# Role adapters on one core: every transfer of the phases on SyncE's queue, h as an image in DRAM, weight sums' transfers spread, tables loaded by place

## The chip, the cores and the metric

The kernel runs on one core of one Trainium2 chip. The metric is the device time of one execution in microseconds (us); the figure for the kernel before is the median of three executions.

## The reference

Two layers, each an adapter with a residual and a layer norm, whose weights are chosen per sample by a role (three roles; the drawn roles are 1 or 2). All data are float32; x has 128 samples of 128 x 1024.

```python
# one layer; role has one entry per sample, H = 1024, K = 512, R = 3
h = jnp.einsum('bsh,bhk->bsk', hidden_states, W_down[role]) + b_down[role][:, None, :]
h = jax.nn.gelu(h, approximate=False)
u = jnp.einsum('bsk,bkh->bsh', h, W_up[role]) + b_up[role][:, None, :]
y = hidden_states + u
mean = jnp.mean(y, axis=-1, keepdims=True)
var = jnp.mean(jnp.square(y - mean), axis=-1, keepdims=True)
yn = (y - mean) * jax.lax.rsqrt(var + LN_EPS)
return yn * gamma[role][:, None, :] + beta[role][:, None, :]
```

The second layer takes the first one's result and the same roles.

## The kernel before

**Sorting.** The kernel first counts the roles on the chip and orders the samples so that two of the same role stand side by side. An item is such a pair; 63 items are pairs, and item 63 holds the two samples left over. "Place" is the rank of a role: place 0 is the most frequent role, and weights and tables are stored by place.

**Phases and items.** The work is four phases: Down and Up of layer 0, then Down and Up of layer 1. In each, 64 items pass. Down makes h = gelu(x W_down + b) and stores h in DRAM (tensor hd); Up loads h and x, makes the product with W_up, adds x, normalises and stores to mid (layer 0) or to the result (layer 1).

**Seven products.** A pair is multiplied by Winograd's scheme: seven half-sized products instead of eight. It needs sums of quarters of the data (`winograd_sums`, mostly on GpSimd, POOL in the profile) and of the weights (T1 to T4). The products s1 to s7 of an item (`item_products`) accumulate into banks b, a and e. Bank b is used by s1, s3, s5 and s7 one after the other, and between them ScalarE (ACT) or VectorE (DVE) reads it: s7 may not start before DVE has read what s5 left (`end`, line 550). The sums of weights of the three later phases are made during the first phase by nine jobs (`Sums`, one for each phase and place): four transfers of 512 KB in, four subtractions on DVE (line 209), seven transfers of 512 KB out to DRAM (tensors B and T). They use the memory of tables 0 and 1.

**Layout of x and h.** [...] x is loaded by `quartered` in four pieces of 128 KB for a sample (line 384), into buffers with tag q, and DVE transposes it in blocks of 32 x 32 (line 522). h is stored row by row (line 558), loaded with `quartered` in four pieces of 64 KB for a sample, and transposed in Up (line 589).

**The order.** Every step has a time in a plan (`at`), in units; items start 7 units apart, so two of them overlap. The steps are written in the order of these times, and each engine keeps to that order. The times only set the order: an engine runs as early as the waits allow. In the plan of Down, the two halves of h are stored 10.7 and 12.5 units after the item's start; x is loaded 19 units ahead of an item in the first phase (fewer for the first four items) and 11.9 ahead in the third, and transposed 8.8 ahead.

**Queues.** A transfer is issued by SyncE (SP) or by ScalarE (ACT), each in its own order. Before, ACT issues the stores of h and the tables (bias, gamma, beta, three places in one go); SP issues the rest. Each transfer of either queue is given one of eight completion semaphores in turn (DMAHW0 to DMAHW7 in the listing of the order), and is issued only when the transfer before it on that semaphore has landed. So at most eight are under way, those of ACT among them.

**The end.** The last item's result is stored by `finish_last` in four pieces, three by SP (line 650) and one by ACT (line 656). Since the row of the result is known only at run time, each store into it waits for the one before.

Of the kernel before, what the change touches and what calls it, by code (L numbers as in the profile page):

```python
# [10 lines left out]
F32 = mybir.dt.float32  # L11
# [15 lines left out]
def kernel(  # L27
# [24 lines left out]


    nc = tc.nc
    B, S, H = x.shape
# [56 lines left out]
    def table(v, which):  # L112
        n = v.shape[1]
        t = tables[:, which].rearrange("p (r n) -> p r n", r=R)[:, :, 0:n]

        def load(places=range(R)):
            for k in places:
                r = reg(role_of, k, [ENG.Activation], R - 1)
                nc.scalar.dma_start(t[:, k], v[ds(r, 1), :].to_broadcast((P, n)))

        return t, load
# [53 lines left out]
    class Sums:  # L175
# [21 lines left out]

        def load(self):
            role = reg(role_of, self.k, [ENG.SP], R - 1)
            rows = self.w.shape[1] // NQ  # L200
            for q in range(NQ):
                src = self.w[ds(role, 1), ds(q * rows, rows), :]
                nc.sync.dma_start(
                    self.whole[ts(q, SQ)], src.rearrange("o (m i) c -> i (o m) c", i=SQ)
                )

# [7 lines left out]
    class Phase:  # L214
        def __init__(self, layer, up):
            self.layer, self.up, self.weights = layer, up, {}
            self.vectors = layers[layer][3:] if up else layers[layer][1:2]

        def load_bias(self, which):
            self.next_bias, load, self.subtract = bias_table(self.vectors[0], which)  # L220
            load()

        def set_bias(self):
            self.subtract()
            self.bias = self.next_bias

        def load_gamma(self):
            self.gamma, load = table(self.vectors[1], 1)
            load()

        def load_beta(self):
            self.beta, load = table(self.vectors[2], 2)
            load()

# [193 lines left out]
    def item_products(item, cols):  # L428
# [9 lines left out]
        if n < NPAIR:  # L438
# [61 lines left out]
    class Down:  # L500
# [18 lines left out]
        def prepare(self):  # L519
            self.a = flat("t", 3, "xT" + self.tag).rearrange("p (s j c) -> p s j c", s=2, c=P)  # L520
            for s in range(2):
                nc.vector.transpose(  # L522
                    self.a[:, s].rearrange("p j (a t) -> p j a t", t=SQ),
                    self.xq[s].rearrange("p a (j i) -> p j a i", i=SQ),
                )
                if s == 0 and self.early:
                    first_sum("T1", 0)
# [28 lines left out]
        def finish(self):  # L556
            return [
                (t, lambda s=s: nc.scalar.dma_start(hd[self.n][s], self.h[s]))
                for s, t in enumerate((10.7, 12.5))
            ]  # L560

    class Up:
# [63 lines left out]
        def finish_last(self):  # L626
# [3 lines left out]
            o = [flat("q", 4, f"o{self.tag}_{s}", H) for s in range(2)]  # L630
            out_row = lambda s: out[ds(self.out_at[s], 1)].rearrange("o s h -> (o s) h")
            row = lambda t, s, cols: t[:, ds(self.places[s], 1), cols].rearrange("p o n -> p (o n)")
# [14 lines left out]
            def stored(s, cols, queue):  # L647
                y, v = o[s][:, cols], mv[s][:, 2:3]
                nc.vector.scalar_tensor_tensor(y, y, v, row(self.ph.beta, s, cols), ALU.mult, ALU.add)  # L649
                queue.dma_start(out_row(s)[:, cols], y)  # L650

            def stored_beside():
                y, v = o[0][:, left], mv[0][:, 2:3]
                nc.scalar.mul(y, y, v)
                nc.gpsimd.tensor_tensor(y, y, row(self.ph.beta, 0, left), ALU.add)
                nc.scalar.dma_start(out_row(0)[:, left], y)

# [11 lines left out]
        def finish(self):  # L669
# [3 lines left out]
            for s in range(2):  # L673
# [22 lines left out]
                def stored(s=s, box=box, row=row):  # L696
# [6 lines left out]
                    if self.layer == 0:  # L703
                        dst = mid[self.n][s]
                    else:
                        i = reg(perm, 2 * self.n + s, [ENG.SP], B - 1)
                        dst = out[ds(i, 1)].rearrange("o s h -> (o s) h")
                    nc.sync.dma_start(dst, o)

# [17 lines left out]
    for k, ph in enumerate(phases):  # L727
# [36 lines left out]
        if k + 1 < len(phases):  # L764

            nxt = phases[k + 1]
            if nxt.up:
                at(base - 2 * SLOTS, lambda nxt=nxt: nxt.load_bias(0))
                at(base - 2 * SLOTS + 3, nxt.set_bias)
                at(base - 2 * SLOTS, nxt.load_gamma)  # L770
                at(base + 2 * SLOTS - 1, nxt.load_beta)
            else:


                at(base + 1.6, lambda nxt=nxt: nxt.load_bias(0))
                at(base + 4.2, nxt.set_bias)
                at(base + SLOTS * NI // 2, lambda nxt=nxt: nxt.load_bias(2))
                at(base + SLOTS * NI // 2 + 3, nxt.set_bias)

# [28 lines left out]
    at(-29, lambda: load_bias([0]))  # L808
    at(-29, lambda: load_rows(0, 0, nc.scalar, ENG.Activation, (0, 1)))
# [56 lines left out]
```

## Time and profile before

| what | value |
|---|---|
| median of three executions (range) | 3200.29 us (3198.03 to 3203.08) |
| the profiled execution, its own time | 3195.31 us |
| its span, first to last instruction | 3193.5 us |
| granted TensorE clock, mean | 0.994 |
| busy: PE / DVE / ACT / POOL | 3123.4 / 1762.3 / 1199.2 / 1767.4 us |
| DMA busy share, about: Down of layer 0 / Up of layer 0 / Down of layer 1 / Up of layer 1 | 0.76 / 0.71 / 0.47 / 0.67 |

PE is the matmul side of TensorE. A line of the view of waits reads: engine and line that waited, what it waited for, us in total, how often, the longest. A line of the timeline reads: start in us, length in us, engine, line, operation, output from input, how many in a row, and in brackets how long the engine had been idle and what ended that. SPq and ACTq are the two engines' instructions that issue transfers. A wait for a tensor named hd by SP is a wait for a store of h to land.

### The profile page before, as it was taken

The numbers are of one execution on the slowest core, as the hardware profiler recorded it, in microseconds if no ns is written. First come the engines' busy times: TensorE is split into PE (matmuls) and PEld (weight loads), VectorE is DVE, ScalarE is ACT, GpSimd is POOL, SyncE is SP. The second block draws the span as 40 slices with busy tenths as digits, with TensorE's granted clock in tenths as the row PEclk, the third lists the DMA queues.
The fourth block names the chain that finished last, engine by engine and source line by source line (L and its number), as shares of the span: only waits on it lengthen the run. The fifth ranks groups of instructions, "written<-read, shape, count | busy, mean of one in ns | idle before, by whom it ended". The sixth has DMA issues, their size and how long they took to land. (4 is left out here: it accounts for less than half of the span.)

```text
span 3193.5 us, 43475 instructions
## 1 busy us (share of the span) xinstructions
PE 3123.4 (98%) x10806; PEld 2054.9 (64%) x10806; DVE 1762.3 (55%) x2792; ACT 1199.2 (38%) x2814; POOL 1767.4 (55%) x1396
## 2 busy tenths in 40 slices
PE   8999999999999999999989999999999999999997
PEld 6888888888544444444478888888884444444443
DVE  4433333333577777777752332323226777787777
ACT  1222222222344545454432222222224545455453
POOL 3444434443467676777664433344435777677775
PEclk9999999999999999999999999999999999999999
DMA  6877777778887767677796444544468766666664
GB/s 154 204 215 212 202 206 203 207 203 230 273 252 214 220 211 218 210 223 213 224 258 172 133 129 132 142 130 135 128 182 290 242 211 223 219 211 227 211 220 165
DMA packets 447840, 642.87 MB, mean 201 GB/s; under 512 B 48497, under 2 KB 318322, under 8 KB 447602
## 3 DMA queue, kind: packets, MB, share of 16 engines
q1 hardware_dynamic: 406130, 559.85, 60.1%
q10 hardware_dynamic: 41472, 80.23, 7.2%
q8 instruction: 102, 1.67, 0.2%
q14 instruction: 136, 1.11, 0.1%
HBM read 405.54 MB, written 234.36 MB: 200 GB/s over the span
## 5 line engine op out<-in xcount | busy, mean ns | idle before, releaser
L407 PE MATMUL bu<-wall,hTu 128*128 (+1 forms) x2048 | 926.4, 594 | 17.3 <-DVE xu L611 12.2
L407 PEld LDWEIGHTS bu<-wall,hTu 128*128 128x128 f32 x2048 | 387.4, 190 | 513.9 <-issue 427.5
L398 POOL TENSOR_TENSOR Sd<-xTd 128x512 f32<-128x512 f32 x125 | 167.0, 1336 | 848.1 <-DVE xTd L522 776.1
L689 POOL TENSOR_TENSOR varu<-varu,mhalf 128x1 f32<-128x1 f32 x254 | 333.7, 1314 | 395.9 <-ACT varu L688 373.9
L522 DVE STREAM_TRANSPOSE xTd<-xqd 128x1024 f32<-128x1024 f32 x256 | 307.5, 1229 | 399.2 <-PE bd L407 259.9
L407 PE MATMUL bd<-wall,xTd 128*128 (+1 forms) x2080 | 493.1, 380 | 13.6 <-DVE hd L550 11.0
L692 DVE SCALAR_TENSOR_TENSOR ou<-xu,meanu,tables 128x1024 f32<-128x1024 f32 x254 | 326.2, 1284 | 317.6 <-ACT ou L687 317.6
L407 PE MATMUL eu<-wall,hTu 128*128 (+1 forms) x1040 | 488.4, 592 | 2.6 <-DMA wall<-T 1.5
L407 PE MATMUL bd<-wall,Sd 128*128 (+1 forms) x2016 | 477.9, 380 | 4.9 <-ACT hd L546 4.9
L407 PEld LDWEIGHTS bd<-wall,xTd 128*128 128x128 f32 x2080 | 395.3, 190 | 72.7 <-DVE hd L550 14.4
L407 PEld LDWEIGHTS bd<-wall,Sd 128*128 128x128 f32 x2016 | 384.0, 191 | 59.2 <-issue 7.0
L551 ACT ACTIVATE hd<-hd 128x256 f32<-128x256 f32 x382 | 157.5, 416 | 593.7 <-DVE hd L550 593.7
L407 PEld LDWEIGHTS eu<-wall,hTu 128*128 128x128 f32 x1040 | 197.3, 190 | 251.3 <-issue 239.6
L683 ACT ACTIVATE partu<-statu 128x2 f32<-128x2 f32 x254 | 51.7, 203 | 740.6 <-DVE xu L620 740.6
L700 POOL TENSOR_TENSOR ou<-ou,tables 128x1024 f32<-128x1024 f32 x127 | 298.9, 2354 | 0.0
L687 ACT ACTIVATE ou<-xu,meanu 128x1024 f32<-128x1024 f32 x254 | 291.7, 1148 | 13.7 <-DMA mid<-ou 5.2
L407 PE MATMUL ed<-wall,xTd 128*128 (+1 forms) x1072 | 254.0, 380 | 0.0
L398 POOL TENSOR_TENSOR hTu<-hTu 128x256 f32<-128x256 f32 x126 | 203.7, 1616 | 82.6 <-DVE hTu L589 63.1
L407 PE MATMUL ad<-wall,xTd 128*128 (+1 forms) x1008 | 240.0, 381 | 4.9 <-DMA wall<-in_L_cond_W_down_dram 4.9
L407 PE MATMUL ed<-wall,Sd 128*128 (+1 forms) x1008 | 238.1, 379 | 0.0
L407 PE MATMUL au<-wall,hTu 128*128 (+1 forms) x504 | 236.8, 592 | 0.0
L407 PEld LDWEIGHTS ed<-wall,xTd 128*128 128x128 f32 x1072 | 204.7, 191 | 28.7 <-ACT ou L687 0.2
(110 smaller groups left out, 3312.3 us busy)
## 6 DMA issues: line engine op xcount, KB each, us to landing
xqd<-in_x_dram SPq DMA_DIRECT2D x512, 128.0 KB, 3.2
hd<-hd ACTq DMA_DIRECT2D x256, 256.0 KB, 2.6
hqu<-hd SPq DMA_DIRECT2D x1024, 64.0 KB, 4.0
xu<-in_x_dram SPq DMA_DIRECT2D x128, 512.0 KB, 5.3
mid<-ou SPq DMA_DIRECT2D x128, 512.0 KB, 4.3
xqd<-mid SPq DMA_DIRECT2D x512, 128.0 KB, 3.4
xu<-mid SPq DMA_DIRECT2D x128, 512.0 KB, 5.7
out_dram<-ou SPq DMA_DIRECT2D x126, 512.0 KB, 4.9
```

What stands on the lines that cost most here:

```text
L398: engine.tensor_tensor(dst[:, 1], a11, a21, ALU.subtract)
L407: nc.tensor.matmul(ps[:, 0:cols], a[:, j], w.rhs(r, j, cols), start=start and j == 0, stop=j == n - 1, skip_group_check=True,)
L522: nc.vector.transpose(self.a[:, s].rearrange("p j (a t) -> p j a t", t=SQ), self.xq[s].rearrange("p a (j i) -> p j a i", i=SQ),)
L551: nc.scalar.activation(y, y, AF.Gelu)
L683: nc.scalar.mul(part, self.stat[:, s], -1.0 / H)
L687: nc.scalar.activation(box["o"], self.x[:, s], AF.Square, bias=m, accum_out=v)
L689: nc.gpsimd.tensor_tensor(v, v, mhalf[:, 0:1], ALU.pow)
L692: nc.vector.scalar_tensor_tensor(box["o"], self.x[:, s], box["m"][:, 0:1], row(self.ph.gamma), ALU.add, ALU.mult)
L700: nc.gpsimd.tensor_tensor(o, o, row(self.ph.beta), ALU.add)
```

## The change

- **h.** The tensor hd now holds for each sample an image of what Up wants to have in memory: the store puts each row's four pieces of 128 elements (512 bytes) where the load then finds 512 contiguous elements (2 KB) for each partition. The load is one transfer of 512 KB for the two samples (first three items of a phase) or two of 256 KB, in place of eight of 64 KB. The store moves from ACT to SP. So that the rows come out in this order, the transpose in Down now reads every eighth element and writes every fourth; the rows of W_down are assigned to partitions to match, which makes the 4 (or 8) rows that a partition receives contiguous in DRAM.
- **Weight sums.** A job's four loads stand 3.5 units apart instead of together, its seven stores 3.5 units apart, and its subtractions later.
- **Tables.** Bias, gamma and beta are loaded by SP; place 0 when all three were loaded before, places 1 and 2 some items into the phase. Only the first bias of place 0 stays with ACT.
- **Result.** The stores into the result are declared independent of each other.
- **First item.** Its product with T1 (s4, bank e) comes before the one with B21 (s2, bank a).

```diff
@@ stores and loads of h, transposes, rows of W_down
-    hd = [dram.tile([2, S, K], F32, tag=f"hd{n}", name=f"hd{n}") for n in range(NI)]
+    hd = [dram.tile([2, S * K], F32, tag=f"hd{n}", name=f"hd{n}") for n in range(NI)]
...
             for s in range(2):
                 nc.vector.transpose(
-                    self.a[:, s].rearrange("p j (a t) -> p j a t", t=SQ),
-                    self.xq[s].rearrange("p a (j i) -> p j a i", i=SQ),
+                    self.a[:, s].rearrange("p j (t a) -> p j a t", t=SQ),
+                    self.xq[s].rearrange("p a (i j) -> p j a i", i=SQ),
                 )
...
         def finish(self):
-            return [
-                (t, lambda s=s: nc.scalar.dma_start(hd[self.n][s], self.h[s]))
-                for s, t in enumerate((10.7, 12.5))
-            ]
+            def store(s):
+                dst = hd[self.n][s : s + 1].rearrange("o (q p c) -> p (o q) c", q=NQ, p=P)
+                nc.sync.dma_start(dst, self.h[s].rearrange("p (q c) -> p q c", q=NQ))
+
+            return [(t, lambda s=s: store(s)) for s, t in enumerate((10.7, 12.5))]
...
+            src = hd[self.n].rearrange("s (p n) -> p s n", p=P)
             if self.m < 3:
-                hq = flat("q", 4, "hq" + self.tag, H)
-                self.hq = [hq[:, ts(s, K)] for s in range(2)]
+                hq = flat("q", 4, "hq" + self.tag, H).rearrange("p (s n) -> p s n", s=2)
+                nc.sync.dma_start(hq, src)
+                self.hq = [hq[:, s] for s in range(2)]
             else:
                 self.hq = [flat(f"h{s}", 2, f"hq{self.tag}_{s}", K) for s in range(2)]
+                for s in range(2):
+                    nc.sync.dma_start(self.hq[s], src[:, s])
             self.hq = [t.rearrange("p (a c) -> p a c", a=NQ) for t in self.hq]
-            quartered(self.hq, [hd[self.n][s] for s in range(2)])
...
-            src = w[ds(role, 1), ds(q * H // NQ + k * P, P), :]
+            src = w[ds(role, 1), ds(q * H // NQ, H // NQ), :]
+            src = src.rearrange("o (i m) c -> i (o m) c", i=SQ)
             engine.dma_start(
-                rows_of[k][ts(q, SQ), place].rearrange("p j h c -> p j (h c)"),
-                src.rearrange("o (j i) c -> i (o j) c", i=SQ),
+                rows_of[k][ts(q, SQ), place].rearrange("p j h c -> p j (h c)"), src[:, ts(k, NQ)]
             )
@@ weight sums
+            self.rows = "o (m i) c -> i (o m) c" if up else "o (i m) c -> i (o m) c"
...
-        at(start + 0.25, job.load)
-        for t, name in ((9.25, "B11"), (11.25, "B21"), (13.25, "B22"), (18.25, "T1"), (20.25, "T2"), (22.25, "T3"), (24.25, "T4")):
-            at(start + t, lambda job=job, name=name: job.store(name))
-        for t, name in ((10.3, "T1"), (12.3, "T2"), (15.3, "T3"), (17.3, "T4")):
+
+        for q in range(NQ):
+            at(start + 3.5 * q + 0.25, lambda job=job, q=q: job.load(q))
+        for i, name in enumerate(("B11", "B21", "B22", "T1", "T2", "T3", "T4")):
+            at(start + 3.5 * i + 17.75, lambda job=job, name=name: job.store(name))
+        for t, name in zip((22.3, 24.3, 29.3, 31.3), ("T1", "T2", "T3", "T4")):
@@ tables
-        def load(places=range(R)):
+        def load(places=range(R), queue=nc.sync):
             for k in places:
-                r = reg(role_of, k, [ENG.Activation], R - 1)
-                nc.scalar.dma_start(t[:, k], v[ds(r, 1), :].to_broadcast((P, n)))
+                r = reg(role_of, k, [queue.engine], R - 1)
+                queue.dma_start(t[:, k], v[ds(r, 1), :].to_broadcast((P, n)))
...
+                at(base - 2 * SLOTS, lambda nxt=nxt: nxt.load_bias([0]))
+                at(base - 2 * SLOTS + 3, lambda nxt=nxt: nxt.subtract(place_0))
...
+                at(base - 2 * SLOTS, lambda nxt=nxt: nxt.load_gamma([0]))
+                at(base + 2 * SLOTS - 1, lambda nxt=nxt: nxt.load_beta([0]))
+                later_places(6 * SLOTS - 1, nxt.load_gamma)
+                later_places(7 * SLOTS - 1, nxt.load_beta)
+                later_places(10 * SLOTS - 1, lambda p, nxt=nxt: nxt.load_bias(p))
@@ result, first item
+    def result(i, y, cols, queue):
+        dst = out[ds(i, 1), :, cols].rearrange("o s h -> (o s) h")
+        store = queue.dma_start(dst, y).ins
+        tc.declare_no_dep(store, group="result", reason="disjoint rows")
+        tc.add_to_no_dep_group("result", store)
...
-            times = (0, 1, 4, 2, 6.5, 6, 8) if item.early else range(0, 14, 2)
+            times = (0, 2, 4, 1, 6.5, 6, 8) if item.early else range(0, 14, 2)
```

More of the change, by code (lines that the diff above doesn't have):

```diff
@@ L196, in __init__, with load @@
             self.to = {name: block(t[:, k]) for name, t in scratch[layer, up].items()}
-        def load(self):
-            role = reg(role_of, self.k, [ENG.SP], R - 1)
+        def load(self, q):
+            if q == 0:
+                self.role = reg(role_of, self.k, [ENG.SP], R - 1)
             rows = self.w.shape[1] // NQ
[L201 to L205, printed above, removed]
+            src = self.w[ds(self.role, 1), ds(q * rows, rows), :]
+            nc.sync.dma_start(self.whole[ts(q, SQ)], src.rearrange(self.rows, i=SQ))
         def sum(self, name):
@@ L217, in __init__, with new_bias @@
             self.vectors = layers[layer][3:] if up else layers[layer][1:2]
-        def load_bias(self, which):
-            self.next_bias, load, self.subtract = bias_table(self.vectors[0], which)
-            load()
+            if up:
+                self.gamma, self.load_gamma = table(self.vectors[1], 1)
+                self.beta, self.load_beta = table(self.vectors[2], 2)
+        def new_bias(self, which):
+            self.next_bias, self.load_bias, self.subtract = bias_table(self.vectors[0], which)
         def set_bias(self):
-            self.subtract()
             self.bias = self.next_bias
[L227 to L233, printed above, removed]
     area = flat("s", 3, "sorting", 1792)
@@ L630, in finish_last @@
             o = [flat("q", 4, f"o{self.tag}_{s}", H) for s in range(2)]
-            out_row = lambda s: out[ds(self.out_at[s], 1)].rearrange("o s h -> (o s) h")
             row = lambda t, s, cols: t[:, ds(self.places[s], 1), cols].rearrange("p o n -> p (o n)")
@@ L649, in stored @@
                 nc.vector.scalar_tensor_tensor(y, y, v, row(self.ph.beta, s, cols), ALU.mult, ALU.add)
-                queue.dma_start(out_row(s)[:, cols], y)
+                result(self.out_at[s], y, cols, queue)
             def stored_beside():
@@ L655, in stored_beside @@
                 nc.gpsimd.tensor_tensor(y, y, row(self.ph.beta, 0, left), ALU.add)
-                nc.scalar.dma_start(out_row(0)[:, left], y)
+                result(self.out_at[0], y, left, nc.scalar)
             return [
@@ L703, in stored @@
                     if self.layer == 0:
-                        dst = mid[self.n][s]
+                        nc.sync.dma_start(mid[self.n][s], o)
                     else:
                         i = reg(perm, 2 * self.n + s, [ENG.SP], B - 1)
-                        dst = out[ds(i, 1)].rearrange("o s h -> (o s) h")
-                    nc.sync.dma_start(dst, o)
+                        result(i, o, slice(0, H), nc.sync)
                 steps += [(t, squares), (t + 1.3, scaled), (t + 3.1, stored)]
@@ L766 @@
             nxt = phases[k + 1]
+            later_places = lambda time, load: [
+                at(base + time + SLOTS * 2 * i, lambda k_=k_: load([k_])) for i, k_ in enumerate(range(1, R))
+            ]
+            place_0, others = slice(0, 1), slice(1, R)
             if nxt.up:
-                at(base - 2 * SLOTS, lambda nxt=nxt: nxt.load_bias(0))
+                at(base - 2 * SLOTS, lambda nxt=nxt: nxt.new_bias(0))
+                at(base - 2 * SLOTS, lambda nxt=nxt: nxt.load_bias([0]))
+                at(base - 2 * SLOTS + 3, lambda nxt=nxt: nxt.subtract(place_0))
                 at(base - 2 * SLOTS + 3, nxt.set_bias)
-                at(base - 2 * SLOTS, nxt.load_gamma)
-                at(base + 2 * SLOTS - 1, nxt.load_beta)
-            else:
-                at(base + 1.6, lambda nxt=nxt: nxt.load_bias(0))
+                at(base - 2 * SLOTS, lambda nxt=nxt: nxt.load_gamma([0]))
[3 more added lines that the diff above has]
+                later_places(10 * SLOTS - 1, lambda p, nxt=nxt: nxt.load_bias(p))
+                at(base + 14 * SLOTS - 1.9, lambda nxt=nxt: nxt.subtract(others))
+            else:
+                at(base + 1.6, lambda nxt=nxt: nxt.new_bias(0))
+                at(base + 1.6, lambda nxt=nxt: nxt.load_bias([0]))
+                at(base + 4.2, lambda nxt=nxt: nxt.subtract(place_0))
                 at(base + 4.2, nxt.set_bias)
-                at(base + SLOTS * NI // 2, lambda nxt=nxt: nxt.load_bias(2))
-                at(base + SLOTS * NI // 2 + 3, nxt.set_bias)
+                later_places(5 * SLOTS - 0.6, lambda p, nxt=nxt: nxt.load_bias(p))
+                at(base + 10 * SLOTS - 1.9, lambda nxt=nxt: nxt.subtract(others))
+                half = base + SLOTS * NI // 2
+                at(half, lambda nxt=nxt: nxt.new_bias(2))
+                at(half, lambda nxt=nxt: nxt.load_bias())
+                at(half + SLOTS, lambda nxt=nxt: nxt.subtract())
+                at(half + SLOTS, nxt.set_bias)
             if k == 0:
@@ L807 @@
     ph.bias, load_bias, subtract = bias_table(ph.vectors[0], 2)
-    at(-29, lambda: load_bias([0]))
+    at(-29, lambda: load_bias([0], nc.scalar))
     at(-29, lambda: load_rows(0, 0, nc.scalar, ENG.Activation, (0, 1)))
```

## The prediction

> **What bounds the kernel now.** I read the page's busy time first, then the waits of PE, then the timeline around the longest of them.
>
> ```profile
> span 3193.5 us, 43475 instructions
> PE 3123.4 (98%) x10806; PEld 2054.9 (64%) x10806; DVE 1762.3 (55%) x2792; ACT 1199.2 (38%) x2814; POOL 1767.4 (55%) x1396
> ```
>
> TensorE is busy for 98% of the span, and the change takes no product away. So what it can win is PE's idle time: 3193.5 - 3123.4 = 70.1 us, and no more, except that matmuls just after a stall run slower. Of the 70, 13.4 us lie in the first 50 us (PE is busy for 36.6 of them), and 18.3 after the last product, which ends at 3175.2 in the timeline. Some 38 us lie between. Whose waits they are:
>
> ```profile
> PE bu L407 <- DVE xu L611: 12.2, 8, 7.4
> PE bd L407 <- DVE hd L550: 11.0, 8, 2.4
> PE ad L407 <- DMA wall<-in_L_cond_W_down_dram: 4.9, 1, 4.9
> PE bd L407 <- ACT hd L546: 4.9, 2, 3.4
> PE bu L407 <- ACT bu L425: 3.2, 3, 1.7
> PE bd L407 <- ACT bd L425: 2.6, 1, 2.6
> ```
>
> Six short lists, each with one place. I go through them with the part of the change that touches them.
>
> **Part 1: SP's queue in the first phase (row of 11.0 us).** The eight waits lie between 93 and 738 us, two at the loads of W_down for places 1 and 2 and the others about 72 us or a multiple of it apart, which is six items, the period of the weight-sum jobs. In the waits of the stretch 100 to 800 us, SP and DVE say why:
>
> ```profile
> SPq L212 <- DMA hd<-hd: 94.5, 26, 6.0
> SPq L203 <- DMA hd<-hd: 81.7, 11, 9.6
> ...
> DVE xTd L522 <- DMA xqd<-in_x_dram: 91.3, 40, 4.8
> DVE tables L209 <- DMA B<-tables: 26.6, 9, 4.2
> ```
>
> SP stands before a job's loads and stores until a store of h has landed, because the eight semaphores are shared with ACT, whose store waits for gelu. Then it issues 2 MB of loads and the delayed x together, x arrives late, DVE waits for it in its transposes, line 550 stands behind them, and s7 waits for line 550. After the change the listing of the order has, for an item, eight loads of x, a store of h, one transfer of a job, the other store of h, one transfer of a job. SP now waits for gelu at the store itself, which frees it no earlier than before; what is gained is that at most 512 KB of weights stand between two such points. Is x in time? In this phase it is planned 19 units ahead and transposed 8 to 9 ahead. An item takes 12.03 us (third phase, 769.9 us for 64), so a unit is 1.72 us. x of item m+5 follows the second store of item m, which goes out at 13.3 units (s7 ends at 13); eight issues at 0.51 us and 3.3 us to land make 7.4 us, with 512 KB ahead of it (1.9 us at the 270 GB/s of the fullest slices) 9.3 us, or 5.4 units: 18.7 against a transpose at 27. Fourteen us to spare, so even the 2 MB of W_down rows (still in two lumps of four) fit. The subtractions come seven units or more after their last load. I take 10 of the 11.0 us; ends 6 and 11.
>
> **Part 2: tables off ACT (row of 4.9 us).** At the end of both Down phases ACT issues three or six tables, and each waits for a free semaphore:
>
> ```profile
> 2355.45 6.56 ACTq L119 DMA_DIRECT2D tables<-in_L_cond_ln_w_dram  x3
> 2360.57 3.95 SPq L384 DMA_DIRECT2D hqu<-hd  x6
> 2362.05 0.37 ACT L546 COPY hd<-bd 128x256 f32<-128x256 f32 x1 [9.38 <-DMA tables<-in_L_cond_ln_w_dram]
> ```
>
> Behind it stands the copy of line 546 that PE waits for (3.4 us here, 1.5 us at 785 us). These issues leave ACT, so 4.9 us go (ends 3 and 4.9). SP then waits instead: behind it stand h's next store and the first loads of the next phase, planned 9 to 16 units before use, and it carries one place instead of three at that point.
>
> **Part 3: h's loads (row of 12.2 us less its 7.4).** In Up, eight loads of 64 KB take SP 3.7 to 7.9 us to issue with their waits, and DVE's transpose waits for them in 54 cases, 24.3 us in total. Two loads of 256 KB need about 1 us to issue, so those waits should go. PE's share is the seven short waits, 12.2 - 7.4 = 4.8 us. Some come of DVE's own order behind ACT's line 687, so I take 3.3 (ends 0 and 4.8). Leftover item: the 3.2 us of line 425 stay.
>
> **Part 4: the end.**
>
> ```profile
> 3182.41 2.89 DVE L649 SCALAR_TENSOR_TENSOR ou<-ou,last_mv,tables 128x512 f32<-128x512 f32 x3
> 3184.00 6.87 SPq L650 DMA_DIRECT2D out_dram<-ou  x3
> 3188.36 0.37 ACTq L656 DMA_DIRECT2D out_dram<-ou  x1
> ```
>
> The data of the last store are there at 3182.41 + 2.89 = 3185.30, but it is issued at 3190.54, the end of its three less 0.33, because each store waits for the one before. Without these waits it goes at about 3185.4: 5.1 us, with nothing beside it. ACT's store can leave at 3183.5. Ends 4 and 5.5. The same waits in the middle of the phase are hidden by PE.
>
> **Part 5: the start.** PE waits 4.91 us from 24.0 to 28.95 for W_down's second rows. The product with T1, which stood behind it (8 records, 2.8 us), needs only first rows and sums that are ready at 26.1. It now runs inside that wait. It takes up to 3.75 us at the cold clock that the product with B21 shows here, so it may end 0.9 us late: 2.0 us, ends 1 and 2.8.
>
> **Part 6: what is added.** No row shows a strided transpose. The row at hand is the contiguous one:
>
> ```profile
> 2350.63 2.37 DVE L522 STREAM_TRANSPOSE xTd<-xqd 128x1024 f32<-128x1024 f32 x2 [3.09 <-PE bd L407]
> 2350.99 0.33 ACTq L558 DMA_DIRECT2D hd<-hd  x1
> ...
> 2355.82 0.43 DVE L550 TENSOR_TENSOR hd<-bd,hd 128x256 f32<-128x256 f32 x1 [2.82 <-PE bd L407]
> ```
>
> [...] Twice would still fit: 2.5 us more in a gap of 2.82 us before line 550, which in turn has three product steps (5.2 us) until s7 needs it; the sums on POOL end at 2358 and would end at 2361, before 2362.7, when the item starts. Cover is missing only where Up turns into Down and DVE is nearly full (38 to 40 us of 50). There two to four transposes would cost up to 5 us. I take 1.5 us.
>
> h's stores become four times as many packets, of 512 instead of 2048 bytes. In the trace's packet records, 512-byte packets (loads) take 31 ns on average, 2048-byte stores of h 88.5 ns. An item's store goes from 256 x 88.5 = 22.7 us to 1024 x 31 = 31.7 us of engine time, 9 us of the 16 x 12.03 = 192.5 that an item has: 5 points of DMA share, 0.76 to 0.81 and 0.47 to 0.52; Up loses the same 5 points. [...] In the third phase x has less room than in the first: second store of h at 2350.99, eight issues 4.1, landing 3.3, so 2358.4, or 2360.3 with 512 KB of weights ahead, against a transpose at 2350.63 + 12.03 = 2362.7. It holds by 2.4 us.
>
> **What stays.** The longest stall, at 1594 us where Up of layer 0 ends, is not touched:
>
> ```profile
> 1596.45 1.15 ACT L687 ACTIVATE ou<-xu,meanu 128x1024 f32<-128x1024 f32 x1 [5.23 <-DMA mid<-ou]
> ...
> 1602.24 6.45 PE L407 MATMUL bu<-wall,hTu 128*128 x8 [7.45 <-DVE xu L611]
> ```
>
> ACT needs a buffer whose store of mid stands in the queue behind 1.5 MB of x and weights; the listing has the same transfers in the same order after the change. I count nothing, with 0 and 10 us (7.4 and the 2.6 of line 425) as ends.
>
> **Sum.** 10 + 4.9 + 3.3 + 5.1 + 2.0 - 1.5 = 23.8 us. The profiled execution took 3195.31 us, so it would take 3171.5; it lies 5 us below the median of the runs. From that median: 3200.29 - 23.8 = 3176.5 us.
>
> **Rivals.** (a) *The long stall falls too*, because SP, freed of 16 small loads, issues the store of mid earlier: 10 us more, 3166. Against it: that store waits for DVE's result, not for SP. (b) *The wait moves from ACT to SP.* h's stores hold SP until gelu ends, so x and weights come late at the joins and in the third phase: parts 1 and 3 win half (5 and 1.5 us) and a few stalls of 1 to 3 us arise, 8 us in all. 23.8 - 6.8 - 8 = 9 us: 3191. For it: SP is now one line for everything. Against it: SP already waited for those stores (595 us in the whole run) through the semaphores. (c) *Slower: the small writes.* No row shows 512-byte writes to DRAM. In the first phase the engines have 24% of 192.5 us free and h's own 13.9%: 73 us for 1024 packets, 71 ns each. Above this the phase is bound by transfers, and each 10 ns costs 0.64 us in each of some 55 items, 35 us. At 78 ns all the gain is gone; at 100 ns the phase loses 102 us: 3200 - 24 + 102 = 3278. For it, the missing row; against it, 2048-byte writes cost no more than 2048-byte reads (85 and 87 ns, medians). A transpose above 5 us would do the same; four times the row is far.
>
> **How the numbers follow.** Forecast 0.63, (a) 0.15, (b) 0.14, (c) with the slow transpose 0.08. The best ends give 11 + 4.9 + 4.8 + 5.5 + 2.8 + 10 = 39, so 3161; a little below it for matmuls that no longer run slowly after a stall: 3158. The worst ends give 6 + 3 + 0 + 4 + 1 - 5 = 9 us, 3191, which is (b) too; some of its width takes it to 3194. (c) is left out. A measurement of this kernel tells about 0.2%, 6.4 us, from no change. Faster: 0.63 + 0.15 and most of (b), 0.88; same 0.04; slower 0.08.
>
> **What would show it.** No wait of PE for line 550 between 90 and 740 us, and DVE's transposes waiting for PE instead of x; no ACT wait for tables; DVE's line for h's transposes without waits for a load; the last store 5 us earlier; the stall near 1594 still there. It is wrong if the transposes' mean rises above 2.5 us, if the share of DMA in the first phase goes above 0.9, or if PE's waits in the third phase, where there are none now, appear.

## The result and the profile after

The changed kernel takes 3152.05 us (median of five executions, 3151.07 to 3155.05) against 3200.29 before: a ratio of 0.985, 95% interval 0.9836 to 0.9865. It gained 48.2 us where the forecast gained 23.8, so the direction was right and the size was half of it. The profiled execution took 3151.07 us, 44.2 less than that of before; the other 4 us of the 48.2 are that the profiled execution of before lay 5 us below its median and this one 1 us.

The busy time of the page, changed kernel:

```profile
span 3149.3 us, 42330 instructions
PE 3112.8 (99%) x10806; PEld 2056.5 (65%) x10806; DVE 1976.1 (63%) x2795; ACT 1201.7 (38%) x2814; POOL 1793.0 (57%) x1396
```

PE's idle time fell from 70.1 to 36.5 us, by 33.6. The same 10806 products are also busy for 10.6 us less. About half of this is matmuls that no longer run slowly after a stall, which the forecast left out of its sum; the rest is delay between products that the page counts as busy. DVE is busy for 214 us more.

The view of waits, PE, changed kernel:

```profile
PE bu L410 <- DVE xu L618: 5.5, 1, 5.5
PE bd L410 <- ACT bd L428: 4.0, 1, 4.0
PE ed L410 <- DVE xTd L402: 3.0, 1, 3.0
...
PE bd L410 <- ACT hd L549: 0.8, 1, 0.8
```

(Lines have moved: 410, 549, 553, 618 and 428 are the 407, 546, 550, 611 and 425 of before.) The row of 11.0 us for line 550 is gone, as is that of 4.9 for the copy behind the tables. Of the row of 12.2 us for Up's additions only its one long stall is left. But the row of 3.2 us for line 425, which was to stay, is gone as well, and with it all other short waits in Up.

To see where the time went I use the starts of the product records: how long from the start of a phase's first product to that of its last, the few that are interleaved at a join left out. One stage's figures can be set against another kernel's without asking who waited:

| us | before | after | less |
|---|---|---|---|
| Down of layer 0 | 794.2 | 774.8 | 19.4 |
| join to Up (overlap of the two) | 12.3 | 10.5 | 1.8 |
| Up of layer 0 | 781.2 | 768.4 | 12.8 |
| join to Down of layer 1 | 13.6 | 16.6 | -3.0 |
| Down of layer 1 | 769.9 | 765.8 | 4.1 |
| Up of layer 1 | 770.8 | 766.0 | 4.8 |
| after the last product's start | 18.9 | 14.7 | 4.2 |

The two Up phases and the join ahead of the first gave 19.4 us, 2.4 of them at the long stall. That is where the forecast had 3.3.

The end, from the timeline of the changed kernel:

```profile
3135.34 10.38 SPq L377 DMA_DIRECT2D out_dram<-ou  x5
...
3142.48 2.89 DVE L655 SCALAR_TENSOR_TENSOR ou<-ou,last_mv,tables 128x512 f32<-128x512 f32 x3
3143.52 0.40 ACTq L377 DMA_DIRECT2D out_dram<-ou  x1
```

The last data are there at 3142.48 + 2.89 = 3145.37, and the last of the five stores is issued at 3145.72 - 0.33 = 3145.39: nothing waits for an earlier store. The 5.2 us between data and issue are gone; from the issue to the end of the span are now 3.9 us instead of 3.0, so 4.2 are left.

The transposes on DVE, from the groups by form, before and after:

```profile
L522 DVE STREAM_TRANSPOSE xTd<-xqd 128x1024 f32<-128x1024 f32 x256 | 307.5, 1229 | 399.2 <-PE bd L407 259.9 <-DMA xqd<-in_x_dram 103.7 <-DMA xqd<-mid 22.4
L589 DVE STREAM_TRANSPOSE hTu<-hqu 128x512 f32<-128x512 f32 x256 | 173.5, 698 | 26.0 <-DMA hqu<-hd 24.3 <-issue 0.2
```
```profile
L525 DVE STREAM_TRANSPOSE xTd<-xqd 128x1024 f32<-128x1024 f32 x256 | 518.2, 2088 | 354.4 <-PE bd L410 275.1 <-POOL Sd L404 32.3 <-DMA hd<-hd 15.4
L596 DVE STREAM_TRANSPOSE hTu<-hqu 128x512 f32<-128x512 f32 x256 | 167.3, 690 | 4.0 <-DMA hqu<-hd 3.9
```

A transpose of x takes 2088 ns on average instead of 1229, and its waits for x to arrive are no longer among the reasons shown (103.7 us before). The contiguous transposes of h are as they were, but wait 3.9 us for their load instead of 24.3.

### The profile page after: what moved, and what is told of

It reads as the page before. It is cut to its first block, busy times and chain, and to the rows that moved or that the text cites. A ratio compares the mean times of both kernels' runs of the same rounds, so it can differ in the third digit from the quotient of the medians.

```text
span 3149.3 us, 42330 instructions
## 1 busy us (share of the span) xinstructions
PE 3112.8 (99%) x10806; PEld 2056.5 (65%) x10806; DVE 1976.1 (63%) x2795; ACT 1201.7 (38%) x2814; POOL 1793.0 (57%) x1396
## 3 DMA queue, kind: packets, MB, share of 16 engines
q10 hardware_dynamic: 480, 1.57, 0.2%
## 5 line engine op out<-in xcount | busy, mean ns | idle before, releaser
L525 DVE STREAM_TRANSPOSE xTd<-xqd 128x1024 f32<-128x1024 f32 x256 | 518.2, 2088 | 354.4 <-PE bd L410 275.1
```

The source lines that it names most:

```text
L525: nc.vector.transpose(self.a[:, s].rearrange("p j (t a) -> p j a t", t=SQ), self.xq[s].rearrange("p a (i j) -> p j a i", i=SQ),)
```

## The experiments

Each run is the changed kernel with something put back, or something more. All were timed beside the kernel before, whose median there was 3196.9 to 3199.3 us, so a difference of 2 or 3 us between medians is not told from none. The stage columns are worked out from the product records as above, of one execution each. That execution lay 6.0 us above its run's median in split8, 5.5 in hact and 3.5 in rowhlt, in the others within 2.5.

| run | us (range) | Down 0 | Up 0 | Down 1 | Up 1 |
|---|---|---|---|---|---|
| before | 3200.3 | 794.2 | 781.2 | 769.9 | 770.8 |
| after | 3152.1 | 774.8 | 768.4 | 765.8 | 766.0 |
| rowh | 3181.0 (3176.9 to 3184.1) | 775.9 | 788.6 | 764.7 | 775.7 |
| split8 | 3174.6 (3166.5 to 3180.7) | 774.6 | 781.6 | 765.4 | 780.1 |
| tabs | 3163.8 (3163.3 to 3167.5) | 782.2 | 767.9 | 773.0 | 766.0 |
| rowtabs | 3185.3 (3177.3 to 3190.5) | 779.7 | 784.8 | 773.1 | 771.4 |
| hact | 3165.6 (3161.7 to 3171.1) | 793.6 | 769.2 | 765.6 | 766.0 |
| lump | 3153.3 (3151.5 to 3156.6) | 778.2 | 767.9 | 764.8 | 767.1 |
| hactlump | 3181.6 (3179.0 to 3183.1) | 802.9 | 767.9 | 765.8 | 766.0 |
| rowhl | 3199.3 (3187.9 to 3204.7) | 787.3 | 788.0 | 764.7 | 777.9 |
| rowhlt | 3225.5 (3217.9 to 3230.2) | 804.2 | 791.5 | 766.4 | 788.2 |
| ends | 3158.0 (3157.7 to 3158.1) | 777.5 | 769.6 | 765.2 | 766.0 |
| read | 3152.3 (3149.7 to 3153.9) | 776.7 | 766.6 | 765.7 | 766.0 |
| join | 3150.5 (3149.9 to 3151.1) | 776.8 | 767.9 | 765.4 | 766.0 |
| prep | 3151.7 (3150.4 to 3153.9) | 777.7 | 762.1 | 765.1 | 766.0 |
| join2 | 3148.2 (3145.7 to 3151.0) | 774.9 | 760.1 | 764.7 | 766.0 |
| join3 | 3146.5 (3145.3 to 3147.9) | 776.6 | 760.2 | 769.4 | 766.0 |

Down 0 scatters by some 3 us, because the stall of the first item, which is part of it, was 2.2 to 6.0 us long from one run to another.

### Up: how h is loaded

**rowh** undoes the image: h row by row, eight loads of 64 KB for an item, plain transposes.

```diff
-                nc.sync.dma_start(dst, self.h[s].rearrange("p (q c) -> p q c", q=NQ))
+                nc.sync.dma_start(hd[self.n][s], self.h[s])
...
+            quartered(self.hq, [hd[self.n][s] for s in range(2)])
```

> Against the changed kernel (3152). Theory A, the prediction's terms: the image of h is worth 3.3 us in PE's waits, and the plain transposes and big packets give 1.5 back: +2 us, 3154. Theory B, late data of h keeps VectorE behind TensorE through both Up phases, with short stalls of which the waits list only the longest, and matmuls run slower after each: +12 to +17 us, 3164 to 3169, nearly all of it in the two Up phases, and TensorE's busy time up by 3 us or more. Under B, VectorE waits for eight loads of h again (54 waits or so), and the transposes of x fall back to 1245 ns.

It cost 29 us, above both expectations, all in the Up phases (20.2 and 9.7 us) and their joins. **split8** keeps image, transposes and packets, and cuts only the load:

```diff
-                for s in range(2):
-                    nc.sync.dma_start(self.hq[s], src[:, s])
+            for s in range(2):
+                for q in range(NQ):
+                    nc.sync.dma_start(self.hq[s][ts(q, SQ)], src[ts(q, SQ), s])
```

> h's image stays in DRAM, with the same packets of 2 KB, and only its load is cut again into eight transfers of 64 KB, for an item. Theory A, the number of transfers that SyncE issues in Up is what cost the time: nearly all that the row kernel lost comes back, +25 us, 3177, with 20 or so waits of TensorE for line 618 and SyncE waiting for its own transfers before line 584. Theory B, the layout in DRAM (packets of 512 bytes on one side or the other, the transposes) carries it: under +8 us, 3152 to 3160.

It cost 22.6 us, close to theory A: the number of transfers is what carries most of it. The 6 us that rowh costs beyond it are less than the two runs scatter. How the number of transfers costs time is in the waits of DVE and SP in the stretch from 850 to 1550 us, all inside Up of layer 0. Before:

```profile
DVE hTu L589 <- DMA hqu<-hd: 16.0, 33, 1.9
DVE xu L611 <- PE bu L407: 0.8, 1, 0.8
DVE xu L611 <- PE eu L407: 0.5, 1, 0.5
...
SPq L384 <- DMA mid<-ou: 58.8, 56, 1.6
SPq L384 <- DMA xu<-in_x_dram: 41.6, 61, 1.9
```

After:

```profile
DVE xu L618 <- PE bu L410: 21.3, 31, 0.8
DVE xu L618 <- PE eu L410: 10.9, 25, 0.5
DVE hTu L596 <- DMA hqu<-hd: 2.4, 5, 0.8
...
SPq L710 <- POOL ou L706: 439.5, 59, 8.9
```

And the run split8:

```profile
DVE hTu L596 <- DMA hqu<-hd: 14.5, 23, 2.3
...
SPq L584 <- DMA xu<-in_x_dram: 67.6, 73, 2.6
SPq L584 <- DMA mid<-ou: 58.0, 58, 2.4
```

With eight loads for an item, SP stands before them until its own earlier transfers have landed (100.4 us of such waits before, 125.6 in split8, none left in the changed kernel, where SP has time over and waits for POOL's results). So h comes late, DVE loses 14.5 to 16.0 us to it, and in this phase DVE hardly ever catches up with PE: its additions (lines 611 and 618) wait for a product 1.3 us in 700 before, not at all in split8, and 32.2 us after. An engine that is never ahead passes a delay on, small as it is. The short waits of PE, line 425 at the leftover item among them, are these delays.

How much is passed on can be read from one row, the waits of the transposes of h for their loads in the whole execution, against the length of the two Up phases. Before and in rowh it reads:

```profile
DVE hTu L589 <- DMA hqu<-hd: 24.3, 54, 1.9
```
```profile
DVE hTu L592 <- DMA hqu<-hd: 36.5, 57, 3.5
```

| above the changed kernel, us | before | rowh | split8 | rowtabs | rowhl | rowhlt |
|---|---|---|---|---|---|---|
| DVE's waits for h (changed kernel: 3.9) | 20.4 | 32.6 | 26.8 | 22.2 | 29.4 | 43.9 |
| both Up phases (changed kernel: 1534.4) | 17.6 | 29.9 | 27.3 | 21.8 | 31.5 | 45.3 |

In all six, what DVE waits for h and what the phases are longer by agree within 3 us. (rowtabs, rowhl and rowhlt follow below.) In rowh's Up of layer 1, DVE has time over later (34.4 us of waits for PE after 2850 us), but 10.0 us of its waits for h lie ahead of 2500 us, where it has next to none (0.2 us). So the question whether DVE has time over must be put to the stretch in which it is late.

### Tables

**tabs** puts the tables back on ACT, three places in one go.

```diff
-                at(base - 2 * SLOTS, lambda nxt=nxt: nxt.load_bias([0]))
+                at(base - 2 * SLOTS, lambda nxt=nxt: nxt.load_bias(range(R), nc.scalar))
```

> Only the tables go back to ScalarE, three places in one go at the old times. Theory A, the waits' terms: +4.9 us, 3157 (1.5 near 785 us, 3.4 near 2360 us). Theory B, with slower matmuls after the stalls and the leftovers of h's loads gone from the queue: the stall at 2360 is smaller since SP's loads no longer compete for the same semaphores, +1 to +4 us, 3153 to 3156.

11.7 us, more than either theory: the two phases that end with tables are 7.4 and 7.2 us longer. The timeline of tabs at the second place:

```profile
2328.77 2.12 ACTq L122 DMA_DIRECT2D tables<-in_L_cond_b_up_dram  x3
2336.29 3.06 ACTq L122 DMA_DIRECT2D tables<-in_L_cond_ln_w_dram  x3
2339.47 0.37 ACT L549 COPY hd<-bd 128x256 f32<-128x256 f32 x1 [11.13 <-DMA tables<-in_L_cond_ln_w_dram]
```
```profile
2327.12 15.50 SPq L387 DMA_DIRECT2D xqd<-mid  x8
2343.43 0.38 SPq L562 DMA_DIRECT2D hd<-hd  x1
```

ACT stands 11.1 us at its six table loads (9.4 before), while SP takes 15.5 us for eight loads of x. PE waits 5.31 us and then runs slowly for 2.19: 7.5. In the kernel before the same place cost 3.56 + 1.57 = 5.1. **rowtabs** is rowh and tabs together:

> h row by row with eight loads, and the tables on ScalarE as well, so that SyncE carries no table inside Up. The row kernel alone lost 20.2 us in Up of layer 0 and 9.7 in Up of layer 1 against the changed kernel. Theory A, SyncE in Up is full with the eight loads, and tables in the same queue made it worse: the two phases fall back to what they had before the change (781 and 771 us from the first product to the last, 12 us less than in the row kernel), while the two Down phases take 11.7 us more as in the run of the tables alone; 3180 in all. Theory B, tables have no part in it: Up as in the row kernel (788.6 and 775.7), 3192 in all.

Its Up phases (784.8 and 771.4) are 3.8 and 4.3 us shorter than in rowh: theory A fits the second, the first lies between the two. Its Down phases are 3.8 and 8.4 us longer, and its median is 4.3 us above rowh's, within the scatter of the two. So where SP is full with eight loads, tables in its queue lose in Up 8.1 of the 12.2 us that they win in Down; in the changed kernel, where SP isn't full, they cost nothing that the stages show.

### The first phase: queue of h's store, lumps of weights, and the transposes

**hact** issues the stores of h from ACT again; **lump** loads a weight-sum job's four blocks together again; **hactlump** does both.

```diff
-                nc.sync.dma_start(dst, self.h[s].rearrange("p (q c) -> p q c", q=NQ))
+                nc.scalar.dma_start(dst, self.h[s].rearrange("p (q c) -> p q c", q=NQ))
```
```diff
-            at(start + 3.5 * q + 0.25, lambda job=job, q=q: job.load(q))
+            at(start + 0.25, lambda job=job, q=q: job.load(q))
```

> Only the queue of h's stores goes back to ScalarE. Theory A, the shared semaphores were the cause in the first phase: half or more of the 10 us of part 1 come back, as waits of SP for h before the weights' loads, 3157 to 3162. Theory B, the spreading of the weights' transfers is the cause and the queue is nothing: 3150 to 3154. With either, the stores of h wait for semaphores behind 512 KB transfers, but each is on its own engine.

> Only the times of the weight-sum jobs go back: four loads of 512 KB together, in 2 MB lumps. Theory A, spreading them is what took the stalls of the first phase: +8 to +15 us, 3160 to 3167, with waits of TensorE for the eviction after s5 about every 72 us between 90 and 740 us and x late in VectorE's transposes. Theory B, h's store on the one queue took them: under 3 us, 3152 to 3155.

> Both halves of part 1 are undone: h's stores on ScalarE and the weights' loads together. Alone, the queue cost 13.5 us and the lumps 1.1. Theory A, each hides the other's worth (the shared semaphores stop SyncE only when much is asked for at once): the stalls about every 72 us between 200 and 740 us come back, 9.3 us by the profile before, and with them 3168 to 3176. Theory B, the lumps don't matter with either queue: 3164 to 3168.

The lumps alone cost 1.2 us, not told from none (theory B; there is no stall between 90 and 740 us). The queue alone cost 13.6, more than theory A's 5 to 10, and not by the stalls every 72 us at line 553, of which none is back. PE's waits in hact:

```profile
PE bd L410 <- ACT bd L428: 7.6, 2, 4.2
PE bd L410 <- DVE hd L553: 6.2, 3, 2.9
```

By the product records it has stalls of 3.1 and 2.9 us at the loads of W_down (95 and 124 us), of 1.5 at 440 and of 3.5 at 789 us, where the copy of the bias stands on ACT behind a gelu that waits for line 553. With the slow matmuls after three of them (5.2 us) and a first stall that is longer by 2.5, they make up the 18.8 us of its first phase. Both together cost 29.6, twice the sum of the two, and the stalls every 72 us are back, longer than before. SP and PE in hactlump:

```profile
SPq L387 <- DMA hd<-hd: 576.4, 134, 9.8
...
SPq L214 <- DMA hd<-hd: 105.2, 26, 5.9
SPq L207 <- DMA hd<-hd: 81.4, 10, 9.3
```
```profile
PE bd L410 <- DVE hd L553: 22.0, 11, 3.4
```

So either half of part 1 removes most of the stalls every 72 us; only with both undone is the first phase as bad as before. But 802.9 us for this phase is worse than the 794.2 of before, which had both. **rowhl** is hactlump with h by rows as well, so only the tables, the end and the start of the change are left; **rowhlt** adds the slow transposes to rowhl, with what has to go with them: the rows of h lie in DRAM in another order, with the same packets, and the rows of W_down are loaded as in the changed kernel, in fewer and larger packets. No run separates these from the transposes. Shown is the edit of the transposes.

```diff
-                    self.a[:, s].rearrange("p j (a t) -> p j a t", t=SQ),
-                    self.xq[s].rearrange("p a (j i) -> p j a i", i=SQ),
+                    self.a[:, s].rearrange("p j (t a) -> p j a t", t=SQ),
+                    self.xq[s].rearrange("p a (i j) -> p j a i", i=SQ),
```

> h row by row with plain transposes, its store on ScalarE, the weights in lumps: of the change only the tables, the end and the start are left. By the prediction's terms it is 12.0 us faster than before, 3188. Theory A, the slow transposes and the small packets cost time only where x comes late, which the rest of the change hides: Down of layer 0 takes 788 to 791 us here (before: 794.2, less 2 of the start and 1.6 of the tables), against 802.9 in the run with both halves of part 1 undone. Theory B, that run's 802.9 has another cause: about 800 here too. Up of both layers: as in the row kernel, above the 781 and 771 of before, since tables are in SyncE's queue beside eight loads of h.

> The kernel of the run rowhl (h row by row, its store on ScalarE, lumps of weights) with one difference: the transposes of x read every eighth element and write every fourth, as in the changed kernel; the rows of h lie in DRAM in the order in which they then come out, so that packets and the number of transfers stay as in rowhl. Theory A, the slow transposes are what makes a late x dearer: Down of layer 0 takes 798 to 804 us (rowhl 787.3; 802.9 with both halves of part 1 undone), 3210 to 3216 in all. Theory B, the packets of 512 bytes are: 787 to 790 there, 3199 in all. At the join, where VectorE is nearly full, A adds 1 to 5 us.

rowhl has the 787.3 us of theory A in the first phase, but in all it is as slow as the kernel before (ratio 1.000, 0.999 to 1.0009), not 12 us faster: what tables, end and start win is lost again in Up, 788.0 and 777.9 us against 781.2 and 770.8. rowhlt is slower than before (1.0082, 1.007 to 1.0095), 26 us more than rowhl. In the first phase it takes the 804 us of theory A (16.9 more than rowhl), in all 9.5 us more than theory A's upper end; the Up phases are 3.5 and 10.3 us longer too. PE's waits, rowhl and then rowhlt:

```profile
PE bu L410 <- DVE xu L614: 20.9, 18, 7.3
PE bd L410 <- DVE hd L553: 10.7, 9, 2.1
```
```profile
PE bu L410 <- DVE xu L619: 30.2, 27, 9.2
PE bd L410 <- DVE hd L553: 18.5, 10, 3.2
```

The stalls of the first phase are at the same places; their row goes from 10.7 to 18.5 us (1.4 of it in Down of layer 1), and four of them are now long enough to be followed by slow matmuls (8.1 us by the product records, and 2.2 us more of the first phase are the stall of the first item). When x is late, two transposes of 2.1 us instead of 1.2 stand between its arrival and line 553: that fits, but the stalls were not followed one by one. The Up phases, which have no such transposes, are 13.8 us longer, and DVE waits 14.5 us more for h's loads there (table above): h comes later. Why it does, these runs don't show; its order in DRAM differs.

### The transposes and the join

**read** lets the transposes read contiguous elements and keeps only the step of the writes.

```diff
-                    self.xq[s].rearrange("p a (i j) -> p j a i", i=SQ),
+                    self.xq[s].rearrange("p a (j i) -> p j a i", i=SQ),
```

> The transposes of x read contiguous elements again and only write with a step of 16 bytes; h's image in DRAM is kept, the rows of W_down fit the other order. Theory A, the slow transposes cost the 1.5 us that the prediction put on them, at the join of layer 0's Up and layer 1's Down: -1 to -3 us there, 3149 to 3151. Theory B, they are hidden everywhere and the join waits for a transfer: within 1 us of 3152. The mean of a transpose: 1245 ns if the reads' step is what slows it, 2090 if the writes' is, between them if both.

```profile
L525 DVE STREAM_TRANSPOSE xTd<-xqd 128x1024 f32<-128x1024 f32 x256 | 500.7, 2045 | 357.0 <-PE bd L410 275.5 <-POOL Sd L404 35.2 <-DMA hd<-hd 15.4
```

Of the 859 ns that a transpose had gained, 816 stay: the step of 16 bytes in the writes slows it, that of 32 bytes in the reads adds 43 ns to this (the reads' step alone was not run). The kernel's time is the same (theory B).

The stall at the end of layer 0's Up is the largest that the change left. Timeline of the changed kernel:

```profile
1561.28 1.15 ACT L693 ACTIVATE ou<-xu,meanu 128x1024 f32<-128x1024 f32 x1 [4.93 <-DMA mid<-ou]
...
1563.88 4.01 DVE L525 STREAM_TRANSPOSE xTd<-xqd 128x1024 f32<-128x1024 f32 x2
...
1568.58 6.00 PE L410 MATMUL bu<-wall,hTu 128*128 x8 [5.50 <-DVE xu L618]
```

The addition that PE waits for stands on DVE behind the transposes of the next phase's first item, and these behind the scaling that waits for ACT's squares, which wait for a store of mid. **join** lets that store go ahead of 1 MB of x; **prep** moves the transposes behind two additions; **join2** does both; **join3** also copies the next phase's first bias earlier on ACT.

```diff
+                if k == 1 and m >= NI - 2:
+                    rest = -5.4
...
-                places[0], spare = (slots[0], -SLOTS), slots[-1]
+                places[0], spare = (slots[0], -3 * SLOTS), slots[-1]
```
```diff
-            at(base + (-7.2 if ph is phases[2] and m < 3 else prepare), go)
+            if ph is phases[2] and m < 3:
+                prepare = -4.6 if m == 0 else -7.2
+            at(base + prepare, go)
```
```diff
-                    item.SEED = -0.6
+                    item.SEED = -2.7
```

> At the end of layer 0's Up only, the 1 MB of x of the last two items goes behind a store of mid instead of ahead of it, and the first block of weights of the next phase is loaded 14 units earlier. Theory A, the prediction's reading, that store sits behind 1.5 MB in the queue: the stall of 5.5 us and the slow matmuls after it (2.6) go, -5 to -8 us, 3144 to 3147. Theory B, x is then late for the additions of the last two items, or the bias of the next phase sets the end of the stall (it waits 4.0 us now): -2 to +3 us, 3150 to 3155.

> Only the two transposes of the first item of layer 1's Down are moved on VectorE, from ahead of the additions of the last item of Up to behind the second of them. Theory A, two causes stand one behind the other at the join (ScalarE waits for a store of mid, and the transposes wait for x, both ahead of the additions): removing one shows the other, -1 to -4 us, 3148 to 3151. Theory B, the transposes alone were it: -6 to -10 us, 3142 to 3146.

> The transposes moved as in the run before and the store of mid ahead of 1 MB of x as in the join run. Theory A, with both causes gone, the stall of 5.5 us and the slow matmuls go, and of the bias' wait of 4.0 us a part: -7 to -13 us, 3139 to 3145. Theory B, the transfers at the join (2 MB in some 8 us) set the end in any order, and the wait moves to the first product of Down: -3 to 0, 3149 to 3152.

> The run with both causes at the join removed, and the first bias of layer 1's Down copied to its bank two units earlier on ScalarE, ahead of the second squares of an item of Up instead of behind them. Theory A, in the run before that copy stood behind ScalarE's squares, which wait for VectorE: the wait of 7.5 us falls by 4 to 5, 3143 to 3145 in the median. Theory B, the first product waits for the transposes and sums of x anyway: within 1 us of 3148.

join took ACT's wait away, and its median is 1.6 us lower (theory B's range): the transposes then waited for x instead, to the same microsecond (1563.91). prep took 6 us out of Up and gave them to the first product of Down, whose wait for its bias went from 4.0 to 10.5 us; its median is 0.4 lower. With both, the stall in Up is gone, and the median is lower by 3.9 us of theory A's 7 to 13: the bias still waits. join2 and join3, from their timelines:

```profile
1575.40 3.78 PE L410 MATMUL bd<-wall,xTd 128*128 128x256 f32 x8 [7.48 <-ACT bd L428]
```
```profile
1571.66 3.47 PE L410 MATMUL bd<-wall,xTd 128*128 128x256 f32 x8 [2.73 <-ACT bd L428]
```

join3's earlier bias takes 4.7 us off that wait, and as much comes back in the Down phase (769.4 us against 764.7), with three short stalls between 1591 and 1609 us; its median is 1.7 us lower, too little for theory A. The medians, 3148.2 and 3146.5, are 3.9 and 5.5 us below the changed kernel's, and by their ratios to before (0.9842, 0.9829 to 0.9855, and 0.984, 0.9827 to 0.9853) not told from it. They are the fastest here, by little.

**ends** makes the result's stores wait for each other again and puts the first item's products back.

```diff
-        tc.declare_no_dep(store, group="result", reason="disjoint rows")
-        tc.add_to_no_dep_group("result", store)
...
-            times = (0, 2, 4, 1, 6.5, 6, 8) if item.early else range(0, 14, 2)
+            times = (0, 1, 4, 2, 6.5, 6, 8) if item.early else range(0, 14, 2)
```

> The result's stores depend on each other again, and the first item's products go back to their old order. Theory A, the prediction's terms (5.1 and 2.0): +7 us, 3159. Theory B, by the profile of the changed kernel the tail after the last product got 4.2 us shorter and the first stall 2.2 us: +6.4 us, 3158.5. Either way +4 us in the last 20 us, and the rest near 30 us.

+6.0 us, near both theories (7 and 6.4); its span ends 19.6 us after the start of the last product, as against 14.7.

## Why the prediction was off, by its own steps

The stalls below are extra time between the starts of two products; "slow" is the extra time of the matmuls just after one.

| step | forecast | measured | from |
|---|---|---|---|
| Part 1, first phase | 10 | 14.9 | eight stalls 12.3, slow 2.6 |
| Part 2, tables | 4.9 | 6.7 | 1.6, and 3.56 with 1.57 slow |
| Part 3, h's loads | 3.3 | 16.9 | Up 0 10.4 without the long stall, Up 1 4.8, the wait for T1 ahead of Up 0 1.7 |
| Part 4, end | 5.1 | 4.2 | tail 18.9 to 14.7 |
| Part 5, start | 2.0 | 2.8 | 5.07 and 2.68 slow, to 3.20 and 1.77 |
| Part 6 and the joins | -1.5 | -3.9 | bias wait 2.85 to 5.78, new stall 1.0 |
| what stays | 0 | 2.4 | long stall 10.5 to 8.1, slow ones included |
| sum | 23.8 | 44.0 | of 44.2 between the profiles |

**Part 3 is the term that was mis-sized**: 3.3 us forecast, 16.9 measured, 13.6 of the 20 us. Its mechanism was right, and split8 shows it. Its size came from one row of PE's waits, of which a guess was kept. The better figure stood beside it: the 24.3 us that DVE's transposes wait for h, of which 20.4 went. Of it only the short waits in PE's row were taken to reach PE. The other short rows of Up (3.2 for line 425, 1.1 and 1.1 for the additions, 1.5 for T1, 0.5 for POOL) were taken for things of their own, "the 3.2 us of line 425 stay" among them; they had one cause, and all but 0.6 us at the last item went. With the 4.8 they come to 12.2 us that the list of waits showed. Of the other 4.7, some 2.8 are delays too short to be listed; most of the rest is that the starts lie 0.16 us further apart at each listed wait than its row says. What would have told it was in the trace of before: the waits of DVE's additions for PE in this stretch, 1.3 us in 700. An engine that waits that little for the bound one has next to no slack, so what delays it from outside delays PE. (Its 145 us of waits for ACT in the same stretch are not such a delay: they recur in every item, and fell to 110 when h came in time.)

**Matmuls after a stall** were named for the range and given nothing in the sum. They were worth 1.6 us behind the tables, 2.6 in the first phase and 0.9 at the start.

**Part 6** held in the changed kernel, and for the reason given: twice the time was the author's estimate, which no row of the trace of before shows; 1.70 times was measured (2088 ns against 1229), and the cover held. Of the 859 ns the step of the writes alone gives 816 (read), the step of the reads on top of it 43. But the slow transpose was called hidden without a price for the case that x is late. In rowhlt the first phase is 16.9 us longer with it (2.2 of them at the first item; the rest fits the transposes, though no run separates them from the order of the rows), and the kernel is slower than before. In rival (c) it stood that a transpose would have to exceed 5 us to do such harm; there, 2.1 came with it.

**Rivals.** (a) the long stall fell by 2.4 us, not 10; it is two causes one behind the other, as join, prep and join2 show. (b) that SP as one line for everything comes late elsewhere holds where h still needs eight loads: there the tables in its queue lose in Up most of what they win (rowtabs beside rowh), and rowhl as a whole wins nothing. With the image, of the new stalls of 1 to 3 us one of 1.0 came, in the third phase, where the forecast had named it as a sign of being wrong, and PE waits longer for that phase's first bias (table). But SP now stands 850 us (471.6 and 378.3) before stores that wait for POOL, and between 850 and 1550 us it waits for no transfer of its own any more. (c) fails: 512-byte writes took 30 ns on average in the packet records (estimate 31, what the loads of 512 bytes took in the trace of before), and the engines' busy share from 100 to 800 us is 0.79 (0.75 before; forecast 0.81).

**What the parts are worth together.** Undone one at a time they cost 28.9 (image), 29.6 (part 1), 11.7 (tables) and 6.0 us (end and start): 76, though the whole gained 48.2. The parts pay for each other: the image makes transposes dear, which costs nothing only as long as part 1 keeps x early, and it frees SP, without which two thirds of what the tables win is lost again in Up. A sum over separate edits can't see that.

## To carry to other kernels

Before costing a wait by its row, look whether the engine that ends it ever waits for the bound engine in that stage; if not, don't size the change by the bound engine's rows: take what that engine itself waits for the thing that is to change (here 20.4 us went, and the two phases were 17.6 shorter). Ask of every cost that is "hidden" what it adds to a delay when its cover is late, and which other part of the change provides the cover. Where a stall is traced to one cause, look what stands next on the same engine before expecting its time: at the join it took two edits to remove a stall, and a third wait then took most of its place.

## What was not expected of the hardware

- A 32 x 32 transpose on DVE (128 x 1024 float32) takes 1229 ns contiguous (before), 2045 with a step of 16 bytes in its writes (read), and 2088 with 32 bytes in its reads as well (changed kernel).
- Slow matmuls after a stall (extra time between the starts of two products): they go with a granted clock of 0.50, in stretches of 3.4, 6.8 or 10.2 us (before: 3.41 from 123.03 us, 6.83 from 27.46, 10.24 from 1597.59). In the kernel before, the products from 28.95 us on, in such a stretch, start 427 ns apart, those from 40 to 60 us, at a clock of 1.00, 216 ns (medians). There, the stall of 2.1 us at 122.7 us is followed by one from 123.0 to 126.4; that of 2.5 at 96.4 by none. In join2, the row for the stretch after the wait of 7.48 us has the clock ahead of the last two figures, the DMA's:

```profile
1575.40:1579.00 3.60, 3.60 (x9) 2.88 (x10) 3.56 (x3) 1.02 (x1) 3.47 (x2) 0.50 0.06 24
```

Over all 17 traces here, a clock of 0.50 went with one of 147 stalls of 0.6 to 2.0 us (it followed another stall by 2.8 us), with 11 of 24 between 2.0 and 2.9, and with all 16 between 2.9 and 4 and all 37 above 4; as a rule 1.5 to 3.2 us were lost each time.
